# Linear attention and a mixture of experts on one core: the last batch's u projected behind o instead of behind v

## The chip, the cores and the metric

The kernel runs on one core of one Trainium2 chip. A core has five engines that run their own queues of instructions and wait for each other by semaphores: TensorE (matmuls and transposes, into PSUM), VectorE, ScalarE, GpSimd (POOL in the profile) and SyncE (SP, which here only starts DMA transfers). The metric is the device time of one execution in microseconds.

## What is computed

`x` is 4 batches of 512 tokens of 256 numbers, all float32. First comes a gated linear attention with 16 heads of 16, then a mixture of 8 experts of which each token uses 2. Cut to what matters:

```python
def attn(x):                      # x is the layernorm of the input
    q = elu(x @ Wqk + bqk)        # keys are the same: k = q
    v = silu(x @ Wv + bv)
    u = silu(x @ Wu + bu)
    kv = einsum('bhnd,bhne->bhde', k, v)
    out = einsum('bhnd,bhde->bhne', q, kv)
    out = layernorm(out, ln_g, ln_b)
    return (u * out) @ Wo + bo

def ffn(x):                       # x is a layernorm again
    top2 = top_k(x @ gate, 2)     # weights: softmax over the two
    inter = silu(x @ w0[e]) * (x @ w1[e])
    return sum of weight * (inter @ wo[e]) over the two experts e

x = x + attn(layernorm(x))
x = x + ffn(layernorm(x))
```

u is needed only in the product `u * out`, after the second layernorm of its batch.

## The kernel before

**Stages.** `attention(b)` (L255) is a generator that yields after each of its 15 stages, one generator a batch. The loop at L668 runs 28 steps. Batches begin at steps 0, 4, 8 and 12, so up to four batches are in work, each in another stage. The stages, with the names that the profile shows:

- 0: layernorm 1 of `x` (L239 to L246)
- 1: transposes `xTp`, copied by ScalarE to `xT` (L266)
- 2: `qp`, the q projection, Exp on ScalarE, elu on VectorE, giving `kT`
- 3: `vp` (L291), bias and Silu; then `up` (L305), the u projection: for each of two column halves, two matmuls with `xT` as moving operand into a PSUM tile of 128x512, and a Silu on ScalarE (L309) into `uT`
- 4: `knp` (L318), transposes of `kT` back, copied by VectorE (L321)
- 5: `kvp` (L329), times a mask of heads on VectorE (L333)
- 6: `op` (L343), copied by ScalarE to `o` (L347)
- 7: layernorm 2 of `o`
- 8: transposes `oTp`, evicted by ScalarE with gain and bias (L356), times `uT` on VectorE (L360), giving `yT`
- 9: `ap` (L368), the output projection, added to `x` by VectorE (L372); ScalarE's queue starts the store of `x` to `y` (L375)
- 10: layernorm 3, into `hn`; 11: transposes `hTp`, copied by ScalarE to `hT` (L398); 12: `lp` (L406), the gate logits
- 13: MAX8 and FIND_INDEX8 pick two experts a token (L416, L417); 14: `pos` (L430) counts rows by expert, and GpSimd scatters the rows of `hn` to DRAM, sorted by expert, `xg` (L453)

**Expert blocks.** Once batches 0 and 1 are sorted (step 19), `plan` computes on VectorE a table of 9 full blocks of 128 rows ("early"), with `tot` as its input (L462). From step 20 on each step also advances these blocks: SyncE fetches 128 rows from `xg` (L572, behind the loads of `w2` into the arena, L142, that wait for the arena's places), TensorE transposes them (`gp`, L583), ScalarE and VectorE copy the block's two weight matrices to a staging place (L594, ScalarE the first), TensorE runs `hp` (L602) and `eo` (L624), VectorE and GpSimd scale and add the result to `y` in DRAM. After the attention come 8 "last" blocks and 23 "full" ones, without attention beside them.

**Order.** The order of the text is only the start: when the program is built, a scheduler orders the instructions of each engine, so neighbouring stages of different batches are mixed. At run time each engine keeps its order. Silu and Exp stand in different function tables of ScalarE; a table load (`ACT_TABLE_LOAD`, `LoadActFuncSet` in the program) is put in wherever the needed table changes.

**Places.** Long-lived tiles lie in `arena`, 16 places of 128x1024 float32. `att(tag)` (L94) hands out places in turn; the tag "feat" has three, which `xT`, `yT` and `hT` of all batches share, in the order of their stages.

## Time and profile before

| | us |
|---|---|
| median of 3 runs (346.89 to 348.01) | 347.54 |
| the profiled execution | 338.75 |
| its span, first to last instruction | 337.0 |
| TensorE busy with matmuls in the span | 304.0 (90%) |
| VectorE, ScalarE, GpSimd busy | 155.5, 126.6, 114.3 |
| mean clock granted to TensorE | 0.969 of full |

The profile is of one execution, with times in microseconds from the first instruction. A line of the timeline gives start, length, engine, line of the kernel, operation, result and inputs, count, and in brackets the idle time before it with the instruction that ended it. A q behind an engine's name is its sequencer, which starts DMAs. The time of the profiled execution is not that of the unprofiled runs; only differences are carried from one to the other.

### The profile page before, as it was taken

Reading aid. Unit: us, or ns where it says so; the run is one execution under the profiler, and the core shown is the slowest. Engines: PE = TensorE matmul, PEld = TensorE weight load, DVE = VectorE, ACT = ScalarE, POOL = GpSimd, SP = SyncE. Lnnn points to the kernel's source line nnn. Section 1 sums busy time; section 2 is a strip of 40 time slices with the busy share of each in tenths; the row PEclk is TensorE's granted clock in tenths of the full one; section 3 lists DMA queues with packets and bytes.
Section 4 is the critical chain, followed back from the end, with each engine's and each line's share of the span. In section 5 each row is a group of like instructions: output and inputs, shape, how many; then the busy total and the mean of one; then the engine's idle time right before and its main releaser. Section 6 shows DMA issues by size and latency. Waiting matters only on the chain. (4 is left out here: it accounts for less than half of the span.)

```text
span 337.0 us, 5947 instructions
## 1 busy us (share of the span) xinstructions
PE 304.0 (90%) x2068; PEld 272.9 (81%) x2068; DVE 155.5 (46%) x525; ACT 126.6 (38%) x196; POOL 114.3 (34%) x146
## 2 busy tenths in 40 slices
PE   0999999899987879999999999999999999999930
PEld 0467687696777679999999999999999999999920
DVE  4855879779487665346212121323333232323110
ACT  1455828826613264543211121424243433334100
POOL 5410211307327267356333233232223223413230
PEclk9999999999996799999999999999999999999985
DMA  7999112035256642227434342323634434222220
GB/s 214 375 387 386 59 62 64 2 117 167 82 153 229 178 154 72 36 63 218 85 64 63 49 63 49 47 49 48 175 126 64 61 51 63 37 30 24 26 34 0
DMA packets 27871, 35.58 MB, mean 106 GB/s; under 512 B 2848, under 2 KB 22688, under 8 KB 27808
## 3 DMA queue, kind: packets, MB, share of 16 engines
q1 hardware_dynamic: 18960, 22.00, 21.1%
q0 software_dynamic: 6768, 11.08, 17.8%
q10 hardware_dynamic: 2112, 2.10, 1.9%
q8 instruction: 18, 0.29, 0.4%
q14 instruction: 13, 0.11, 0.1%
HBM read 22.89 MB, written 14.37 MB: 111 GB/s over the span
## 5 line engine op out<-in xcount | busy, mean ns | idle before, releaser
L602 PE MATMUL hp_full<-arena 128*128 128x128 f32 x608 | 73.9, 275 | 0.0
L602 PEld LDWEIGHTS hp_full<-arena 128*128 128x128 f32 x608 | 72.3, 192 | 1.0
L633 POOL DMA_INDIRECT out_dram<-ys_full,g_full x16 | 25.3, 1584 | 58.7 <-DVE ys_full L629 31.8
L453 POOL DMA_INDIRECT xg<-hn,idx_i x32 | 32.5, 1014 | 28.6 <-issue 11.1
L624 PE MATMUL eo_full<-arena,it_full 128*128 x152 | 36.1, 380 | 0.9 <-DVE it_full L612 0.9
L602 PE MATMUL hp_early<-arena 128*128 128x128 f32 x288 | 35.0, 275 | 1.7 <-ACT arena L594 1.7
L602 PEld LDWEIGHTS hp_early<-arena 128*128 128x128 f32 x288 | 34.1, 192 | 2.3 <-ACT arena L594 1.9
L602 PE MATMUL hp_last<-arena,w_sb 128*128 128x128 f32 x256 | 31.2, 275 | 0.0
L602 PEld LDWEIGHTS hp_last<-arena,w_sb 128*128 128x128 f32 x256 | 30.5, 192 | 0.4
L624 PEld LDWEIGHTS eo_full<-arena,it_full 128*128 128x128 f32 x152 | 27.4, 190 | 4.0 <-DVE it_full L612 1.0
L594 ACT COPY arena<-w_sb 128x1024 f32 x28 | 29.3, 1047 | 3.5 <-DVE idx_i L439 1.5
L629 DVE TENSOR_SCALAR ys_full<-eo_full,g_full 128x256 f32<-128x256 f32 x19 | 9.2, 484 | 45.2 <-PE eo_full L624 45.2
L586 ACT COPY arena<-gp_full 128x256 f32<-128x256 f32 x19 | 7.1, 372 | 59.6 <-PE gp_full L583 59.6
L261 POOL TENSOR_TENSOR x<-x,bo 128x256 f32<-128x256 f32 x16 | 12.1, 781 | 38.4 <-DVE arena L244 31.2
L612 DVE TENSOR_TENSOR it_full<-s_full,hp_full 128x512 f32<-128x512 f32 x19 | 13.1, 688 | 26.0 <-PE hp_full L602 26.0
L633 POOL DMA_INDIRECT y<-ys_early,g_early x9 | 14.4, 1597 | 22.7 <-issue 9.2
L633 POOL DMA_INDIRECT y<-ys_last,g_last x8 | 12.4, 1549 | 28.5 <-DVE ys_last L629 22.6
L368 PE MATMUL ap<-wo,arena 128*128 128x256 f32 x64 | 16.6, 414 | 3.9 <-DVE arena L360 2.4
L594 DVE COPY arena<-w_sb 128x1024 f32 x28 | 19.3, 690 | 1.3 <-issue 1.1
L368 PEld LDWEIGHTS ap<-wo,arena 128*128 128x128 f32 x64 | 12.9, 209 | 6.7 <-issue 3.1
L624 PE MATMUL eo_early<-arena,it_early 128*128 x72 | 17.1, 381 | 0.2 <-DVE it_early L612 0.2
L273 PE MATMUL qp<-arena,wqk 128*128 128x512 f32 x32 | 16.7, 668 | 0.2 <-ACT arena L266 0.2
(164 smaller groups left out, 456.7 us busy)
## 6 DMA issues: line engine op xcount, KB each, us to landing
w_sb<-in_w_dram SPq DMA_DIRECT2D x16, 512.0 KB, 10.8
arena<-in_w_dram SPq DMA_DIRECT2D x8, 512.0 KB, 4.6
g_full<-xg SPq DMA_DIRECT2D x19, 130.0 KB, 2.1
x<-in_x_dram SPq DMA_DIRECT2D x4, 512.0 KB, 5.5
y<-x ACTq DMA_DIRECT2D x4, 512.0 KB, 3.5
xg<-empty SPq DMA_DIRECT2D x9, 130.0 KB, 3.5
g_early<-xg SPq DMA_DIRECT2D x9, 130.0 KB, 2.4
g_last<-xg SPq DMA_DIRECT2D x8, 130.0 KB, 2.1
```

The costliest lines, as they stand in the source:

```text
L261: nc.gpsimd.tensor_tensor(xb[:, t, :], xb[:, t, :], bo_sb, ALU.add)
L273: nc.tensor.matmul(ps, lhsT=wqk_sb[:, k, bass.ts(c, P)], rhs=xT[:, k, :], start=(k == 0), stop=(k == EC - 1),)
L368: nc.tensor.matmul(ps[:, t - t0, :], lhsT=yT[:, c, bass.ts(t, P)], rhs=wo_sb[:, c, :], start=(c == 0), stop=(c == EC - 1),)
L453: apart(nc.gpsimd.indirect_dma_start(out=xg[:, :], out_offset=bass.IndirectOffsetOnAxis(ap=idx_i[:, t, k : k + 1], axis=0), in_=hn[:, t, k ...
L586: nc.scalar.copy(gT, ps)
L594: copy(w[i], hw_sb[i][:, bass.ds(at, OW)])
L602: nc.tensor.matmul(ps[:, m, :], lhsT=w[i][:, bass.ds(k * M + m * P, P)], rhs=gT[:, k, :], start=(k == 0), stop=(k == EC - 1),)
L612: nc.vector.tensor_tensor(it, s, ps, ALU.mult)
L624: nc.tensor.matmul(ps, lhsT=it[:, m, :], rhs=w2_sb[:, bass.ds(at + m * E, E)], start=(m == 0), stop=(m == MC - 1),)
L629: nc.vector.tensor_scalar(ys, ps, g[:, E : E + 1], None, ALU.mult)
L633: ins = nc.gpsimd.indirect_dma_start(out=whole[:, :] if full else y[:, :], out_offset=bass.IndirectOffsetOnAxis(ap=g[:, E + 1 : E + 2].bit ...
```

## The change

The body of the u projection becomes a local function `project`. Batches 0 to 2 call it where it stood, behind v (stage 3). Batch 3 (`LATE = 3`) calls it behind o (stage 6). So `xT` of batch 3 is read three stages longer, and its place must stay untouched: the places of the tag "feat" are now listed one by one in `FEAT`. In the order of the turns these are xT0, xT1, yT0, xT2, hT0, yT1, xT3, hT1, yT2, hT2, yT3, hT3.

```diff
+    LATE = 3
...
+    FEAT = [0, 1, 2, 0, 1, 2, 1, 0, 2, 0, 2, 1]
+
     def att(tag):

-        i = turns[tag] % COUNT[tag]
+        i = FEAT[turns[tag]] if tag == "feat" else turns[tag] % COUNT[tag]
         turns[tag] += 1
...
+        def project():
+
+            for c in range(EC):
+                ps = psum.tile([P, N], F32, tag="a", name=f"up_{b}_{c}")
+                for k in range(EC):
+                    nc.tensor.matmul(
+                        ps, lhsT=wu_sb[:, k, bass.ts(c, P)], rhs=xT[:, k, :],
+                        start=(k == 0), stop=(k == EC - 1),
+                    )
+                nc.scalar.activation(uT[:, c, :], ps, AF.Silu, bias=cols_sb[:, 1, c : c + 1])
...
-
         uT = att("uT").rearrange("p (c n) -> p c n", c=EC)
-        for c in range(EC):
-            ps = psum.tile([P, N], F32, tag="a", name=f"up_{b}_{c}")
-            for k in range(EC):
-                nc.tensor.matmul(
-                    ps, lhsT=wu_sb[:, k, bass.ts(c, P)], rhs=xT[:, k, :],
-                    start=(k == 0), stop=(k == EC - 1),
-                )
-            nc.scalar.activation(uT[:, c, :], ps, AF.Silu, bias=cols_sb[:, 1, c : c + 1])
+        if b < LATE:
+            project()
         yield
...
             nc.scalar.copy(o[:, t0 : t0 + 2, :], ps)
+        if b >= LATE:
+            project()
         yield
```

The number of matmuls and of VectorE, GpSimd and SyncE instructions that run stays the same; GpSimd and SyncE keep their order. In the built program the order of TensorE and ScalarE around the move changes so (batch numbers added; "table" is a table load):

```
TensorE before: vp3, up3, lp1, oTp2, knp3, ap2 and kvp3 mixed, pos1, op3, hTp2, tot, lp2, oTp3, ap3, gp, pos2, gp, hp, hp, hTp3, gp, hp
TensorE after:  vp3, lp1, oTp2, knp3, ap2, kvp3, pos1, op3, up3, hTp2, tot, lp2 and oTp3 mixed, ap3, gp, pos2, gp, hp, hp, hTp3 and gp mixed, hp

ScalarE before: table, v3, u3, oTp2, table, two1, store x2, op3, hn2, hTp2, o3, oTp3, two2, gp, store x3, weights, gp, hn3, weights, table, s, hTp3
ScalarE after:  table, v3, oTp2, table, two1, store x2, op3, hn2, table, u3, hTp2, o3, oTp3, table, two2, gp, weights, store x3, gp, table, s, hn3, weights, hTp3
```

ScalarE thus runs two table loads more. On VectorE both copies of knp3 now stand before the two products of batch 2 with u; of batch 3's statistics for layernorm 2, less stands before the end of batch 2's layernorm 3; and the first MAX8 of batch 2, which waits for lp2, stands in the middle of the plan of the early blocks, with the plan's rest and the products of batch 3 with u behind it.

## The prediction

> **What bounds the kernel now.** I read the page first: the 40 slices (8.4 us each), then the group of the work that moves.

> ```profile
> PE   0999999899987879999999999999999999999930
> ...
> PEclk9999999999996799999999999999999999999985
> ...
> L305 PE MATMUL up<-arena,wu 128*128 128x512 f32 x32 | 14.4, 592 | 0.0
> ```

> TensorE is the bound: nearly full from slice 1 to 37, except slices 11 to 14 (93 to 126 us), where its granted clock also falls to 6 and 7 tenths. The four u projections cost 14.4 us, 3.6 us a batch. The page's chain of waits names only the last scatter (0.4% of the span), so the reading must be by stage. I went to TensorE's timeline on both sides of the weak stretch (start, length, engine, line, operation, count, idle before and releaser).

> ```profile
> 83.73 3.60 PE L305 MATMUL up<-arena,wu 128*128 128x512 f32 x8
> 87.16 1.85 PE L406 MATMUL lp<-gate,arena 128*128 128x8 f32 x16
> 88.86 1.07 PE L252 MATMUL oTp<-ident,arena 128*128 128x128 f32 x8
> 89.77 1.04 PE L318 MATMUL knp<-ident,arena 128*128 128x128 f32 x8
> 91.19 1.10 PE L368 MATMUL ap<-wo,arena 128*128 128x256 f32 x4 [0.38 <-DVE arena L360]
> ...
> 97.53 2.03 PE L343 MATMUL op<-arena 128*128 128x128 f32 x16
> 102.60 1.07 PE L252 MATMUL hTp<-ident,hn 128*128 128x128 f32 x8 [3.04 <-DVE hn L244]
> 103.51 0.29 PE L462 MATMUL tot<-count,ones 128*128 128x8 f32 x2
> 104.23 3.64 PE L406 MATMUL lp<-gate,arena 128*128 128x8 f32 x16 [0.44 <-ACT arena L398]
> 107.73 1.95 PE L252 MATMUL oTp<-ident,arena 128*128 128x128 f32 x8
> 111.15 5.29 PE L368 MATMUL ap<-wo,arena 128*128 128x256 f32 x16 [1.47 <-DVE chosen L417]
> ...
> 119.64 3.84 PE L602 MATMUL hp_early<-arena 128*128 128x128 f32 x32 [1.70 <-ACT arena L594]
> ```

> To be seen: after batch 3's o (97.53), TensorE waits 3.04 us for batch 2's third layernorm. The same gate matmul then takes 3.64 us instead of 1.85, the transpose 1.95 instead of 1.07. From 119.64 on TensorE is full, so what counts is how much earlier the expert blocks start. Stretches of half a microsecond (length, busy time of each engine, clock, DMA share, GB/s) date the slow clock:

> ```profile
> 104.00:104.50 0.50, 0.27 (x2) 0.27 (x2) 0.50 (x4) 0.50 (x2) 0.50 (x1) 0.65 1.14 431
> 104.50:105.00 0.50, 0.50 (x4) 0.50 (x4) 0.50 (x5) 0.17 (x1) 0.40 (x1) 0.50 0.81 283
> ...
> 114.00:114.50 0.50, 0.50 (x3) 0.41 (x2) 0.00 (x0) 0.00 (x0) 0.00 (x0) 0.61 0.91 281
> ```

> Half clock from about 104.15 (0.65 = 0.3 at full, 0.7 at half) to 114.39: 10.24 us. Its price: gate 3.64-1.85 = 1.8, transposes 1.95-1.07 = 0.9, and 3.24 us of ap's 5.29 at half speed, 1.6. Together 4.3 us on the path into the blocks.

> [...] 10.24 us is 3.0 windows of 3.41. The window ending at 104.15 holds about 2.3 us of idleness (66%) and cost the clock. The one from 117.80, with 1.64 us idle (48%), did not. So the deciding idleness lies between 1.64 and 2.26 us; I take 1.95. [...] gate products and transposes from 62.3 to 66.87, with 1.07 us idle, did not lose it. [...] The trace shows only the load: below, 83.51 + 1.28 is followed by work at 84.80. I take 1.28 us[...].

> ```profile
> 83.51 1.28 ACT L299 ACT_TABLE_LOAD   x1
> 84.80 1.15 ACT L299 ACTIVATE arena<-vz 128x512 f32<-128x512 f32 x2
> 85.86 0.67 ACT L309 ACTIVATE arena<-up,cols 128x512 f32<-128x512 f32 x1
> ...
> 103.60 1.07 ACT L398 COPY arena<-hTp 128x512 f32<-128x512 f32 x2 [0.77 <-PE hTp L252]
> ```

> **The change, part by part.** Times are those of the profiled run (span 337.0, 338.75 us with what lies around it), up to 83.73 the same. The order on each engine is that of the built programs, and durations are those of the same rows now.

> *Taken out at 83.73:* 3.43 us of TensorE (87.16-83.73), and two Silus on ScalarE. Gate to 85.6, oTp to 86.5, knp to 87.4. Here not all is won. In the new VectorE order both knp copies (0.68 each, from 87.04) stand before the two products with u: products at 88.24 and 88.84. ap starts at 89.07, not 91.19: 2.1 us gained, 1.7 us now idle before ap. kvp ends near 94.5, pos starts 94.4 (was 96.50), op runs 95.4 to 97.4. Batch 2's index is ready 2.3 us earlier.

> *Layernorm 3 of batch 2.* It begins at 96.1 (var, was 98.59). Less of batch 3's statistics stand in between than before, so its nt ends at 98.85, not 101.65. The two ScalarE halves of hn end at 100.04.

> *Put in at 97.3:* u, 3.6 us, to 100.9, beside that layernorm. It fills the gap of 3.04 us; hn is ready 0.9 us before u ends, so hTp runs 100.8 to 101.8. On ScalarE, behind hn: one new table load 100.05 to 101.33, two Silus (0.68 each) to 102.65, and only then the copies of hT, to 103.24 and 103.72. This is the cost: the copies are 0.95 us earlier than at 103.60 instead of about 2. TensorE idles 1.25 us before the gate. The second new load (Exp, after the oTp evictions) lies beside VectorE's work; uncovered it would cost 1.28.

> *After that.* At full clock the gate ends 105.4, oTp 106.2, its eviction starts 106.15. VectorE's next wait matters:

> ```profile
> 107.92 0.17 DVE L416 MAX8 best<-lp 128x8 f32<-128x8 f32 x1 [1.24 <-PE lp L406]
> ...
> 110.31 0.69 DVE L360 TENSOR_TENSOR arena<-arena 128x512 f32<-128x512 f32 x1 [1.36 <-ACT arena L356]
> ```

> In the new order the first MAX8 stands in the middle of the plan, so some fourteen small operations behind it (about 2.0 us by their spacing now) wait for the gate: 105.45 to 107.43, then the product to 108.1. ap runs 108.25 to 111.95 (ended 116.44), after 2.05 us idle. SP's queue: the w2 load that waits for oTp goes at 106.3 (109.75), the first early fetch needs the plan's table (108.35) and a register load: 109.2 (110.94), landed at 112.2. The first block's transposes run at 112.25. Its ScalarE weight copy no longer stands behind the y store (issue 117.32, copy 118.54): 113.1 to 114.15. hp_early starts at 114.2, 5.4 us earlier. Then layernorm 3 of batch 3 (nt 117.6, hn on ScalarE to 118.8) stands before the second block's weight copy, 118.85 to 119.9: hp of block two at 119.95 instead of 124.41. That takes back 0.9; the small wait of 0.23 at 126.59 goes. From there TensorE is full, in the same order with the same instructions. Later fetches, scatters and stores keep their distances.

> *Feature places and uT.* Nothing. Each new predecessor was read long before: the last is hT3's, which is xT3, read by u until 100.9, written near 120. uT's place is overwritten by staging only after the product that reads it.

> Sum: 124.41-119.95 = 4.46, plus up to 0.2: 4.5 us, 334.3 by the profiled run. That run is 8.8 us under the median of the three shown (347.54); I carry the difference over: **343.0 us**. Two bounds: without the clock drop the old chain itself would reach block two near 124.41-4.3 = 120.1, so the gain is almost all clock. And a half-clock window in the new gaps costs 3.4/2 = 1.7.

> **The rivals.**
> 1. *The clock falls once all the same.* Of the new gaps, 2.05 us before batch 3's ap exceeds my threshold and 1.7 before batch 2's ap nears it. [...] 4.5-1.7 = 2.8 us: 344.7.
> 2. *Nothing measurable.* The timed runs before mostly kept the full clock: [...] shorter work in TensorE then only moves waits to VectorE and ScalarE. [...] Gain 0: 347.5. The same comes out if the idle stretch from 101.8 and thin work costs the clock up to ap (3.9 us back, 346.9).
> 3. *Slower: the drop moves into the new kernel.* The table load and Silus hold hT's copies, the plan waits behind the gate, and ap's gap grows to 2.05 us[...]. If most earlier runs had no drop and the new ones have one at that gap, 1.7 us is added: 349.2. It decides where fewer than half of the old runs lost the clock.

> **How the numbers follow.** Forecast 0.52 (range 341.8 to 344.2), rival 1 0.22, rival 2 0.14, rival 3 0.12. About 0.3% (1.0 us) can be told from no change. Faster: the first two, 0.74; same 0.14; slower 0.12. Range: a microsecond of my stage sums below the forecast, up to the edge of rival 2: 341.7 to 346.6.

> **What would show it.** Right: no wait above 1 us between op and up of batch 3, PEclk 9s in slices 13 and 14, batch 2's gate at 1.9 us, hp_early near 114 and equal gaps from there. Wrong: half clock from about 104 again, hp_early later than 117, or block two's weights much later than 120[...].

## The result

| | us |
|---|---|
| the kernel before, beside it | 347.88 (20 runs, 345.79 to 349.90) |
| the changed kernel | 351.38 (20 runs, 347.00 to 354.87) |
| ratio, without its 6 slowest runs | 1.0069 [1.0045, 1.0093] |
| forecast | 343.0 (341.7 to 346.6) |

Six of the 20 runs of the changed kernel are in a slower state, and without them it is slower by 0.7%, or 2.4 us (the medians of all runs differ by 3.5 us); the forecast had it 4.5 us faster. The profiled execution of the changed kernel took 353.07 us (span 351.3), one of its longer ones, so it serves only to show where to look; a shorter one, at 346.94 us, comes below. It looks unlike the profile of before in more than the place of u. The page, work in 40 slices (now of 8.8 us) and the granted clock:

```profile
PE   0999899899696988996999999999999999999930
...
PEclk9999999999896698999699999999999999999995
```

```profile
80.25 3.62 PE L305 MATMUL vp<-wv,arena 128*128 128x256 f32 x16
83.70 1.85 PE L415 MATMUL lp<-gate,arena 128*128 128x8 f32 x16
...
90.79 5.13 PE L377 MATMUL ap<-wo,arena 128*128 128x256 f32 x16 [3.27 <-DVE arena L369]
...
100.44 3.60 PE L293 MATMUL up<-arena,wu 128*128 128x512 f32 x8
103.88 1.04 PE L255 MATMUL hTp<-ident,hn 128*128 128x128 f32 x8
...
108.86 3.16 PE L415 MATMUL lp<-gate,arena 128*128 128x8 f32 x14 [1.74 <-issue]
111.87 1.52 PE L255 MATMUL oTp<-ident,arena 128*128 128x128 f32 x6
114.77 6.77 PE L377 MATMUL ap<-wo,arena 128*128 128x256 f32 x16 [1.38 <-DVE arena L369]
...
129.16 2.05 PE L611 MATMUL hp_early<-arena 128*128 128x128 f32 x16 [0.22 <-ACT arena L603]
```

To be seen: the move itself works. u stands at 100.44, hTp follows without a wait, and the wait of 3.04 us is gone. But batch 2's output projection waits 3.27 us and runs for the most part at half clock (5.13 instead of 3.7), the gate product is broken by 1.74 us, and batch 3's output projection takes 6.77. The second early block starts at 129.16, later than the 124.41 of the profile before. Why it waits is in the other engines' lines (DVE is VectorE, ACT is ScalarE), at 83 to 90 and at 167 us:

```profile
82.95 0.68 DVE L310 TENSOR_TENSOR vz<-vp,bv 128x512 f32<-128x512 f32 x1
87.21 0.69 DVE L310 TENSOR_TENSOR vz<-vp,bv 128x512 f32<-128x512 f32 x1 [3.58 <-PE knp L325]
87.82 0.16 DVE L425 MAX8 best<-lp 128x8 f32<-128x8 f32 x1
90.06 1.28 DVE L369 TENSOR_TENSOR arena<-arena 128x512 f32<-128x512 f32 x2
...
167.50 0.60 ACT L664 ACTIVATE s_early<-hp_early 128x512 f32<-128x512 f32 x1 [8.01 <-remote]
167.59 0.48 DVE L638 TENSOR_SCALAR ys_early<-eo_early,g_early 128x256 f32<-128x256 f32 x1 [5.64 <-remote]
```

The second vz needs only the v product, which ended at 83.87, and starts 3.3 us later. "remote" marks a wait that no instruction of the trace ended. The profile of before has no such wait. So there are two questions: does the change gain where these late starts are missing, and what do they cost each kernel?

### The profile page after: what moved, and what is told of

Same layout as the page of the kernel before. It is cut to its first block, busy times and chain, and to the rows that moved or that the text cites. A ratio compares the mean times of both kernels' runs of the same rounds, so it can differ in the third digit from the quotient of the medians.

```text
span 351.3 us, 5948 instructions
## 1 busy us (share of the span) xinstructions
PE 312.5 (89%) x2068; PEld 278.8 (79%) x2068; DVE 155.9 (44%) x525; ACT 129.0 (37%) x198; POOL 113.0 (32%) x146
## 5 line engine op out<-in xcount | busy, mean ns | idle before, releaser
L611 PE MATMUL hp_early<-arena 128*128 128x128 f32 x288 | 39.4, 292 | 3.7 <-issue 2.8
L462 POOL DMA_INDIRECT xg<-hn,idx_i x32 | 32.3, 1009 | 32.2 <-issue 11.1
L611 PEld LDWEIGHTS hp_early<-arena 128*128 128x128 f32 x288 | 37.6, 207 | 4.8 <-issue 3.1
L377 PE MATMUL ap<-wo,arena 128*128 128x256 f32 x64 | 19.3, 469 | 6.7 <-DVE arena L369 6.7
L377 PEld LDWEIGHTS ap<-wo,arena 128*128 128x128 f32 x64 | 15.0, 241 | 10.4 <-DVE arena L369 6.4
L638 DVE TENSOR_SCALAR ys_early<-eo_early,g_early 128x256 f32<-128x256 f32 x9 | 4.4, 484 | 29.3 <-PE eo_early L633 19.0
```

Of the source, the lines that this page charges most:

```text
L377: nc.tensor.matmul(ps[:, t - t0, :], lhsT=yT[:, c, bass.ts(t, P)], rhs=wo_sb[:, c, :], start=(c == 0), stop=(c == EC - 1),)
L462: apart(nc.gpsimd.indirect_dma_start(out=xg[:, :], out_offset=bass.IndirectOffsetOnAxis(ap=idx_i[:, t, k : k + 1], axis=0), in_=hn[:, t, k ...
L611: nc.tensor.matmul(ps[:, m, :], lhsT=w[i][:, bass.ds(k * M + m * P, P)], rhs=gT[:, k, :], start=(k == 0), stop=(k == EC - 1),)
L638: nc.vector.tensor_scalar(ys, ps, g[:, E : E + 1], None, ALU.mult)
```

## The experiments

Five groups of kernels ran, each group on one chip with the kernel before timed beside it. Ratios are to that kernel, with a 95% interval. The chips fall into two kinds. On three of them (groups 1, 3, 4) the kernel before takes 338.7 to 339.1 us, and no profile has a wait named remote: "prompt" below. On two (groups 2, 5) it takes 346.7 to 346.9, and every profile has them: "late". The profile that the forecast was read from is of the prompt kind. The profile of the changed kernel is of the late kind, and so are, by their times, the timed runs of both kernels in the result. Each chip appears in one group only, so whether the kind belongs to the chip or to the time of its group is not shown.

### Both kernels on both kinds of chip

No edit: the kernel before (first) and the changed kernel (the rest).

> The kernel before, once more, for a second trace of it. Clock theory (the old kernel's timed runs mostly keep the full clock where the first trace lost it): no half-clock stretch, or a short one, between 93 and 126 us, batch 2's gate at 1.9 us. Rival (the first trace is typical, the loss in the changed kernel lies elsewhere): again about 10 us at half clock from near 104. Either way some 9 us over the first trace's 337.0 us span have to show up as waits that the first trace lacks, since the timed runs stand at 347.9.

> The kernel before, for a profile beside the others of this group. Both theories: half clock of three or four windows between batch 3's o and batch 3's ap. If its time lies near 348 instead of 339, the theory that something outside the clock slows the timed runs (late completions on TensorE at the ends of GpSimd's groups of scatters) says that waits named remote or issue of several us appear here too, near 100 to 130 us; the theory of the clock alone says that only the granted clock is lower (under 0.95) and no such waits appear.

> The changed kernel, once more. Clock theory: half-clock stretches start in the waits ahead of batch 2's and batch 3's output projections (near 90 and near 108 us), 10 us or more in all. Table-load theory: full clock in this stretch, but hT's copies late behind the Silus and the product with u late behind the plan; blocks start at 119 or later even so. Stall theory: ScalarE and VectorE start several us after the TensorE result that they wait for, as in the first trace of the changed kernel (4.0 us before the plan's first operation).

> The changed kernel, timed. Clock theory: 0.985 to 0.993 of the kernel before wherever the profile shows no waits named remote; if such waits appear in the profile, 1.003 to 1.010 and a clock at least 0.01 below that of the kernel before.

> The changed kernel, for a profile beside the others of this group. Two kinds of profile have been seen. If waits named remote appear at the ends of GpSimd's groups of eight scatters (near 85, 105, 130 and 160 us), its span is near 345 to 351; if none appears, near 334.

> The changed kernel, for a profile beside the others of this group: span near 333 to 334 without waits named remote, 345 to 351 with them.

| | before | changed | |
|---|---|---|---|
| prompt, group 1 | 339.09 (27 runs) | 335.58 (1) | -3.5 |
| prompt, group 3 | 338.74 (43 runs) | 334.41 (1) | -4.3 |
| prompt, group 4 | 339.13 (19 runs) | 335.19 (1) | -3.9 |
| late, group 2 | 346.88 (57 runs) | 348.73 (20) | 1.005 [1.0028, 1.0073] |

On prompt chips the change gains about what was forecast. There are only single runs of it, but three, each below every run of the kernel before beside it (the lowest are 338.27, 338.25 and 338.56). On the late chip it loses, as before. A lower clock of the changed kernel was expected there, by 0.01 at least; that did not come: the median granted clock of both kernels' runs is 0.957. TensorE's timeline of the changed kernel on the first prompt chip:

```profile
79.50 3.62 PE L305 MATMUL vp<-wv,arena 128*128 128x256 f32 x16
...
88.15 3.72 PE L377 MATMUL ap<-wo,arena 128*128 128x256 f32 x16 [1.54 <-DVE arena L369]
...
99.83 1.04 PE L255 MATMUL hTp<-ident,hn 128*128 128x128 f32 x8
...
101.94 0.39 PE L415 MATMUL lp<-gate,arena 128*128 128x8 f32 x2 [0.95 <-ACT arena L407]
...
102.91 1.63 PE L415 MATMUL lp<-gate,arena 128*128 128x8 f32 x14
104.40 0.85 PE L255 MATMUL oTp<-ident,arena 128*128 128x128 f32 x6
107.95 6.05 PE L377 MATMUL ap<-wo,arena 128*128 128x256 f32 x16 [2.71 <-DVE arena L369]
...
121.65 2.05 PE L611 MATMUL hp_early<-arena 128*128 128x128 f32 x16 [0.26 <-ACT arena L603]
```

Here the waits come close to the forecast: before batch 2's ap 1.54 us (forecast 1.7), before and within the gate 0.95 and about 0.35 (1.25), before batch 3's ap 2.71 (2.05). Only that last ap shows half clock. Times from the start of batch 3's v product to later starts, from the same view of four profiles:

| us from v of batch 3 to | before, prompt | changed, prompt | before, late | changed, late |
|---|---|---|---|---|
| ap of batch 2 | 10.92 | 8.65 | 10.91 | 10.03 |
| gate of batch 2 | 24.49 | 22.44 | 23.95 | 23.80 |
| ap of batch 3 | 31.40 | 28.45 | 31.76 | 32.51 |
| second early block | 45.34 | 42.15 | 45.91 | 45.69 |
| fifth early eo | 72.82 | 69.10 | 74.47 | 74.51 |
| seventh early eo | 83.85 | 80.13 | 90.50 | 92.01 |

Prompt: 2.3 us gained at the first row, 3.2 at the second block, 3.7 from there on. Late: 0.9 at the first row, 0.2 at the second block and nothing at the fifth eo; then 1.5 is lost up to the seventh. The stretch from the fifth to the seventh eo takes 11.03 us in both prompt profiles, 16.03 in the late one of the kernel before (first fence) and 17.50 in that of the changed kernel (second). POOL is GpSimd, L453 or L462 its scatters:

```profile
154.29 1.89 PE L624 MATMUL eo_early<-arena,it_early 128*128 x8
...
158.30 0.98 POOL L453 DMA_INDIRECT xg<-hn,idx_i  x1 [0.30 <-issue]
...
160.53 0.38 PE L602 MATMUL hp_early<-arena 128*128 128x128 f32 x2 [1.09 <-issue]
161.96 3.00 PE L602 MATMUL hp_early<-arena 128*128 128x128 f32 x14 [1.04 <-issue]
162.01 0.60 ACT L655 ACTIVATE s_early<-hp_early 128x512 f32<-128x512 f32 x1 [7.82 <-remote]
162.10 0.48 DVE L629 TENSOR_SCALAR ys_early<-eo_early,g_early 128x256 f32<-128x256 f32 x1 [5.43 <-remote]
...
164.80 1.89 PE L624 MATMUL eo_early<-arena,it_early 128*128 x8
```

```profile
157.58 0.97 POOL L462 DMA_INDIRECT xg<-hn,idx_i  x1 [0.30 <-issue]
...
161.28 3.56 PE L611 MATMUL hp_early<-arena 128*128 128x128 f32 x15 [0.34 <-issue]
161.35 0.60 ACT L664 ACTIVATE s_early<-hp_early 128x512 f32<-128x512 f32 x1 [7.86 <-PE gp_early L592]
161.44 0.48 DVE L638 TENSOR_SCALAR ys_early<-eo_early,g_early 128x256 f32<-128x256 f32 x1 [5.47 <-PE gp_early L592]
...
164.64 2.83 PE L633 MATMUL eo_early<-arena,it_early 128*128 x8
```

VectorE's ys needs eo, which ended near 156.2 in the first fence, and starts at 162.10; TensorE runs single matmuls 0.7 to 1.4 us apart. In the second fence the profile names a transpose of TensorE (gp) as what ended the waits, but it had ended near 160.2, and the starts are the same late ones. The standstill costs both kernels alike: counted from batch 3's v, GpSimd's eight scatters begin after 69.3 and 69.4 us, and TensorE is through after 82.1 and 82.2. There is no head start left to lose at that point. What the changed kernel loses more is half clock: two windows instead of one (its eo takes 2.83 us instead of 1.89). This pair of profiles differs by 0.6 us in span, the medians of the runs on that chip by 1.9, so a part of the loss is in executions that no profile shows.

The first row of the table shows how the move uncovers a late start. On the late chip, the kernel before (two lines) and the changed kernel (two lines):

```profile
85.29 0.69 DVE L296 TENSOR_TENSOR vz<-vp,bv 128x512 f32<-128x512 f32 x1 [2.08 <-PE up L305]
90.73 1.10 PE L368 MATMUL ap<-wo,arena 128*128 128x256 f32 x4 [0.38 <-DVE arena L360]
...
84.59 0.69 DVE L310 TENSOR_TENSOR vz<-vp,bv 128x512 f32<-128x512 f32 x1 [2.11 <-PE oTp L255]
89.12 3.72 PE L377 MATMUL ap<-wo,arena 128*128 128x256 f32 x16 [2.92 <-DVE arena L369]
```

In both, VectorE's second vz starts 1.9 us after v's end (83.44 and 82.71). In the kernel before u keeps TensorE busy until 86.7, and batch 2's ap waits only 0.38 us. Without u there it waits 2.92 (1.54 on the prompt chip, 3.27 in the longer execution above). The rest of the gain goes at the gate: its second part waits 1.65 us for a late copy of hT, where the prompt profile has about 0.35.

### The table loads and Silus

The first kernel leaves out the Silu of batch 3's u and puts Identity in its place, so both new table loads fall away. The second holds the late Silus back behind hT's copies and the layernorm halves of batch 3. The edits are abridged:

```diff
-  nc.scalar.activation(uT[:, c, :], ps, AF.Silu, bias=...)
+  nc.scalar.activation(uT[:, c, :], ps, AF.Silu if b < LATE else AF.Identity, bias=...)
```

```diff
+  waiting.append((c, ps))
...
   layernorm(o, o, b, "2")
+  for c, ps in waiting:
+      tc.keep_in_program_order(nc.scalar.activation(uT[:, c, :], ps, AF.Silu, bias=...))
```

> The changed kernel with the late u left without its Silu (a plain bias instead), so that no function table is loaded for it: two table loads less on ScalarE. Table-load theory: 3 to 4 us faster than the changed kernel, at or below the kernel before (ratio to before 0.995 to 1.000). Clock theory: hT's copies come 1.3 us earlier and the waits in TensorE shrink by as much, 1 to 2 us faster than the changed kernel (ratio 1.002 to 1.006). If the loads cost nothing: ratio 1.007 as the changed kernel.

> The changed kernel with its two late Silus and their table load set behind the copies of batch 2's hT and behind batch 3's layernorm on ScalarE; the matmuls stay where they are. Table-load theory: the gate comes about 2 us earlier, 1.5 to 2.5 us faster than the changed kernel (ratio to before 1.000 to 1.003). Clock theory: the wait ahead of the gate goes, that ahead of batch 3's output projection stays; no more than 1 us faster (ratio 1.004 to 1.008).

On the first prompt chip: 336.39, 0.9908 [0.9880, 0.9935], and 338.16, 0.9967 [0.9951, 0.9984]; the changed kernel itself 335.58. Without the table loads hT's copies start 0.7 us sooner (100.89 in a profile in which v starts at 79.77, against 101.30 and 79.50), but TensorE then waits 1.05 us for batch 3's layernorm on VectorE, and batch 3's ap starts 28.57 us after v, against 28.45. So up to there the first new load costs nothing. The second stands in a wait as well: in the changed kernel it ends at 107.92, and ScalarE's next operation waits for VectorE until 109.38. The final times say less, since this version has a new wait further on (1.57 us instead of 0.64 before the first early block). Held back, the loads did not help, but for another reason: the eviction of oTp starts only 0.6 us later than in the changed kernel, counted from v, while the products of batch 3 with u start 1.8 us later, because the new order on VectorE puts batch 2's whole choice of experts ahead of them. The wait before batch 3's ap grows.

```profile
109.45 6.64 PE L390 MATMUL ap<-wo,arena 128*128 128x256 f32 x16 [4.55 <-DVE arena L382]
```

### Feature places alone, and half a move

`LATE = 4` leaves every u in its place and keeps the list of places. In the other kernel the first column half of batch 3's u goes back behind v:

```diff
-        if b < LATE:
-            project()
+        project(range(EC if b < LATE else 1))
...
-        if b >= LATE:
-            project()
+        if b >= LATE:
+            project(range(1, EC))
```

> The list of feature places alone: every u stays behind v. The forecast puts it at nothing: within 0.5 us of the kernel before, with the same half-clock windows. If a place that is reused too early held up the changed kernel: slower than the kernel before by more than 1 us, with a wait of ScalarE's copies or evictions on TensorE's reads.

> The changed kernel with the first half of batch 3's u (four matmuls, 1.8 us, and its Silu) back behind v and only the second half behind o. Theory: 1.8 us of work lie again ahead of batch 2's output projection, as cover for completions that come late in the first group of scatters (wait there under 0.8 us instead of 1.5 to 2.9), and 1.8 us still fill the wait of 3.04 us, leaving 1.2 us[...]. With late completions: 1 to 3 us less than the changed kernel, at or below the kernel before. Without them: within 1.5 us of the changed kernel. If the clock alone matters and the limit is lower than 1.2 us of idle: half clock from about 102 us as in the kernel before, and its time.

Places alone on a prompt chip: 338.71, 0.9998 [0.9985, 1.0011]: nothing, as forecast. Half a move: 339.78, 1.0026 [1.0010, 1.0042], a miss of what was expected without late completions (within 1.5 us of the changed kernel, 334.41), with four half-clock windows (102.06 to 115.71) like the kernel before. A new order brought a new wait: ScalarE does part of batch 3's layernorm ahead of hT's copies, and the gate product waits 2.98 us. It ran on a prompt chip only, so it says nothing of cover for late starts.

### A longer group of scatters

```diff
-        for t in range(NT):
+        for t in [0, 1, 2, 3] + ([0, 1] if b == B - 1 else []):
             for k in range(TOPK):
                 apart(nc.gpsimd.indirect_dma_start(
```

> The changed kernel in which GpSimd scatters the rows of two of batch 3's four token groups a second time, the same rows to the same places: 12 scatters in a row instead of 8, 1.3 us each, so 5.2 us more, right where the three other engines stood still (156 to 162 us). Nothing is left out. Theory of late completions during GpSimd's scatters: where the standstill is seen at all, it lasts 4 to 6 us longer and ends with the longer group, 2 us behind its end near 166 to 168; the kernel takes 4 to 6 us more than the changed one. Rival, that other traffic (the zero rows that SyncE stores from 154 us, or the instruction fetches) causes it: the standstill stays as long as it was, and what is lost is at most the wait for the rows of the first last block, under 3 us. Where no standstill is seen in the changed kernel, none here either.

> The changed kernel with 12 scatters of batch 3 in a row instead of 8 (5.2 us more, same rows to the same places). Where waits named remote appear in the changed kernel: the standstill of the three engines near 156 to 162 us lasts 4 to 6 us longer and ends about 2 us behind the longer group (late completions during scatters), or it stays as long as it was (other traffic). Where none appear: 0.5 to 1.5 us more than the changed kernel, from the wait for the first last block alone, as seen once.

335.94, 0.9926 [0.9902, 0.9951], and 335.43, 0.9885 [0.9861, 0.9909]: 1.5 and 0.2 us over the single runs of the changed kernel beside them, without any wait named remote. Both landed on prompt chips. Here four scatters more brought no late start; whether scatters cause it on late chips is not shown.

### Useless matmuls in the waits

`spin(ps, n)` puts n matmuls of 128x512 into a PSUM tile that is about to be overwritten, held behind what TensorE was given before. First version, three and five in the changed kernel (ahead of batch 2's and batch 3's ap), six in the kernel before (ahead of hTp):

```diff
+    def spin(ps, n):
+        for _ in range(n):
+            tc.keep_in_program_order(nc.tensor.matmul(
+                ps, lhsT=ident, rhs=wu_sb.rearrange("p c h -> p (c h)"), start=True, stop=True))
...
             ps = psum.tile([P, 2, E], F32, tag="a", name=f"ap_{b}_{t0}")
+            if t0 == 0:
+                spin(ps.rearrange("p t e -> p (t e)"), {2: 3, 3: 5}.get(b, 0))
```

> The changed kernel with useless matmuls of 128x512 (0.45 us each) in the two waits that the change opened: three ahead of batch 2's output projection, five ahead of batch 3's. Clock theory: no half-clock window between 85 and 120 us, batch 3's output projection 3.7 us instead of 6.05, and 1.5 to 2.5 us less than the changed kernel (332 to 334 where that takes 335.6; where that takes 351, 346 to 349). If the lost time is late completions rather than clock: the same as the changed kernel within 0.7 us, and the waits stay.

> The kernel before with six useless matmuls (2.7 us) in the 3.04 us wait between batch 3's o and batch 2's hT transposes; nothing else is added or left out. It prices the clock alone. The working of the forecast says that the whole old chain at full clock reaches the second early block near 120.1 instead of 124.41: 3.5 to 4.5 us less than the kernel before, as fast as the changed kernel or faster. If the waits and not the clock made up the gain: within 1 us of the kernel before.

> The changed kernel with three useless matmuls ahead of batch 2's output projection and five ahead of batch 3's (0.45 us each at full clock). Where no waits named remote appear: full clock from 85 to 120 us, batch 3's output projection 3.7 us instead of 5.7 to 6.05, and 1.5 to 2.5 us less than the changed kernel (332 to 333 where that takes 334.4). Where they appear: within 1 us of the changed kernel in the median, as seen once.

> The kernel before with six useless matmuls in its wait of 3.04 us. Clock theory, where no waits named remote appear: gate product of batch 2 1.85 us instead of 3.64, and 3.5 to 4.5 us less than the kernel before (334.2 to 335.2 where that takes 338.7), that is as fast as the changed kernel. If what the change gained came from work taken off TensorE's path and not from the clock: within 1 us of the kernel before.

| | late | prompt |
|---|---|---|
| changed, filled | 347.88, 0.9997 [0.9969, 1.0025] | 337.27, 0.9939 [0.9921, 0.9958] |
| before, filled | 347.38, 1.0026 [1.0005, 1.0046] | 338.88, 0.9992 [0.9973, 1.0012] |

They were mis-sized: one such float32 matmul is two records of 0.45 us, so 0.9 us; six of them held TensorE 5.3 us in a wait of 3. So none of the gains expected on prompt chips came, and the clock is not priced by them. On the late chip, though, the filled changed kernel is below the changed kernel as it is (0.9997 against 1.005, on the same chip, with intervals that do not meet), so filling its waits helps there; why is not shown. And one profile has a fall of the clock behind a window with little idle time. The changed kernel so filled, on the prompt chip, in stretches of half a microsecond:

```profile
101.50:102.00 0.50, 0.35 (x2) 0.30 (x2) 0.40 (x4) 0.50 (x2) 0.40 (x1) 1.00 0.20 58
102.00:102.50 0.50, 0.04 (x1) 0.03 (x1) 0.50 (x2) 0.50 (x2) 0.30 (x1) 1.00 0.23 83
102.50:103.00 0.50, 0.50 (x5) 0.50 (x6) 0.47 (x3) 0.50 (x2) 0.50 (x1) 1.00 0.62 216
...
105.00:105.50 0.50, 0.50 (x2) 0.15 (x2) 0.50 (x4) 0.49 (x1) 0.50 (x1) 0.54 0.76 266
```

Half clock from 105.04 for 3.41 us. In the window ahead of it, 101.63 to 105.04, TensorE was busy for all but some 0.5 us, with gate products of 8 columns (1.63+0.39) and transposes. That is far less idleness than the 1.95 us of the forecast.

Second version, sized to the waits, so that the order on all other engines stays: in the kernel before two ahead of hTp, one ahead of the gate, two ahead of batch 3's ap; in the changed kernel one ahead of each ap and one ahead of the gate.

> The kernel before with five useless matmuls of 0.9 us each, now of a size that fits the waits (the earlier version held TensorE 2 us too long): two in the wait of 3.04 us ahead of batch 2's hT transposes, one ahead of the gate product (wait 0.24 to 0.44, so up to 0.6 us of delay), two ahead of batch 3's output projection. The order on every other engine is that of the kernel before. Clock theory, where no waits named remote appear: no half clock between 100 and 115 us, gate product 1.85 us, output projection 3.7, and 3.0 to 4.3 us less than the kernel before, about the changed kernel's time. If the gain came from work taken off TensorE's path: within 1 us of the kernel before. Where waits named remote appear: a gain under 1.5 us.

> The changed kernel with three useless matmuls of 0.9 us, one in each of its waits ahead of batch 2's output projection, batch 2's gate product and batch 3's output projection; the order on every other engine is that of the changed kernel. Theory, revised by the last group: a window of 3.4 us without wide matmuls costs the clock, however little of it is idle; here no such window is left. Full clock from 85 to 115 us, batch 3's output projection 3.7 us instead of 5.7 to 6.05, and 1.0 to 2.3 us less than the changed kernel (333 to 334 where that takes 335.2). If the limit is idleness alone (1.95 us): the same, since the longest wait left is 1.8. If one wide matmul in a window is not enough: the half clock stays, within 0.5 us of the changed kernel.

On a late chip, against 346.67: before, filled, 344.86, 0.9961 [0.9943, 0.9979]; changed, filled, 345.40, 0.9973 [0.9947, 0.9999]. The filled kernel before:

```profile
102.50 1.09 PE L254 MATMUL hTp<-ident,hn 128*128 128x128 f32 x8 [1.22 <-DVE hn L244]
...
104.52 1.86 PE L419 MATMUL lp<-gate,arena 128*128 128x8 f32 x16
106.23 1.07 PE L254 MATMUL oTp<-ident,arena 128*128 128x128 f32 x8
107.14 1.88 PE L260 MATMUL ap<-wu,ident 128*128 128x512 f32 x4
111.96 3.72 PE L379 MATMUL ap<-wo,arena 128*128 128x256 f32 x16 [2.93 <-DVE arena L369]
...
123.61 1.95 PE L615 MATMUL hp_early<-arena 128*128 128x128 f32 x16
```

There is no half clock from 100 to 125 us: gate, transposes and ap take their full-clock times. It falls once afterwards, from 127.9 to 131.3, for one window. The second block comes 43.35 us after batch 3's v, against 45.91 on the other late chip. So there full clock alone, with u in its old place, is worth about 2.6 us at that point (two chips compared) and 1.8 in the end, a little more than the 1.5 that was expected at most with late starts.

The filled changed kernel did not reach the full clock that was expected of it:

```profile
106.21 3.15 PE L426 MATMUL lp<-gate,arena 128*128 128x8 f32 x14 [1.72 <-issue]
```

It runs at half clock from 106.06 to 112.88, two windows. The window before had about 0.8 us of the useless wide matmul in it, but 2.0 us of idleness, since the gate waited 1.72 us for a copy of hT that ScalarE started late (at 105.57). So the clock fell behind a window with one wide matmul in it, and the kernel's 345.40 is not its time at full clock. Both filled versions are below the kernel before on that chip, and so below the changed kernel as far as ratios from two chips can be compared (1.005). Neither sized version ran on a prompt chip: what full clock alone would bring there is still an argument, not a run. No version beat the changed kernel's 334.4 to 335.6 there.

## Why the prediction was wrong

- **The failed step: "That run is 8.8 us under the median of the three shown (347.54); I carry the difference over."** The 8.8 us were taken for an offset. They are mostly waits inside the program, in the stretch that the change touches and behind it. From the profile before on a prompt chip to that on a late one (spans 337.1 and 344.6), 0.7 us are lost ahead of batch 3's v, 0.6 from there to the second block, 1.1 to the fifth eo and 5.0 to the seventh. On prompt chips the kernel before takes 338.7 to 339.1 us, and the change gains 3.5 to 4.3; on the late chip it loses 0.5%, in the result 0.7%. So the rule that only differences are carried from the profiled execution to the others does not hold between the two kinds. Why some chips are late stays open.
- **u in front of oTp and knp, "2.1 us gained".** Right on prompt chips (2.3). On the late chip 0.9: u's 3.6 us had covered the late start of VectorE and ScalarE, which stands under the table above. The forecast put this at nothing, and the work that hid it was the work moved away.
- **The gap of 3.04 us, the table loads, the places.** The gap is gone in every profile. A table load took 1.28 us and, where nothing else held it up, the next operation stood 0.01 to 0.02 behind its end (84.80 behind 83.51 + 1.28). Neither load lengthened the way to batch 3's ap on the prompt chip (28.57 us after v without them, 28.45 with them). Places: 0.9998.
- **"So the deciding idleness lies between 1.64 and 2.26 us; I take 1.95."** Wrong. It was the author's estimate from two windows of one profile, and that idleness decides was not shown. In the first prompt profile of the changed kernel the clock falls at 105.87, behind a window with about 0.8 us of idleness. It falls for two windows (6.83 us) instead of none, and batch 3's ap takes 6.05. That is the forecast's first rival, one window longer than it was priced. The kernel before had four windows (13.65 us) in that chip's profile, not the three of the profile read, so the change saved two windows there instead of three. At the second block it gains 3.2 us and not 4.5, and it would be less if the kernel before had lost only what the profile read shows. That the sum came near the forecast on prompt chips is in part luck.
- **"hp_early starts at 114.2" and block two at 119.95.** With v 0.77 us earlier in the profile on the first prompt chip, that is 113.4 and 119.2; it measured 116.15 and 121.65, late by 2.7 and 2.5, mainly ap's 2.3 us of half clock and 0.7 us more of wait.
- **Slower.** The third rival said that the drop moves into the gaps of the new kernel. In the profile at 353.07 it does (5.13 and 6.77 us for the two ap), but the gaps are as long as they are because of late starts, which no rival had. In the execution at 346.94 the half clock around the move lasts three windows, against four in the kernel before on that chip, so in that execution the clock at the move is not what makes the changed kernel slower. Why its runs on late chips lose 0.5 to 0.7% at large stays open in part.

## What to carry to other kernels

Where the profiled execution and the timed runs differ by more than the expected gain, find the difference first: the profile may be of another kind of execution, and a stage read in it does not carry over by subtraction. Before work is moved out of a place, ask which waits of the other engines it covers there, also those that this profile doesn't show. And idle time alone did not tell here when TensorE's clock falls: it fell behind windows of 3.41 us with 0.45 and 0.8 us of idleness, and stayed full behind another with 0.8 us. Look at what runs in such a stretch, too.

## What was not expected of the hardware

- Two kinds of chip for one program, 338.7 to 339.1 us and 346.7 to 346.9. In all seven profiles of the slower kind the page gives no landing time for any transfer and some waits are named remote; in all thirteen of the other kind most landing times are there (2.0 to 2.1 us for the fetch of a full block, 130 KB) and no wait is named so. Whether the missing records and the late starts have one cause is open.
- On late chips ScalarE and VectorE start some 2 to 6 us after the end of the TensorE work that they need, near the ends of GpSimd's four groups of eight scatters: in the kernel before 85.29, 109.82, 132.42 and 162.10 us on VectorE; the groups end at 85.5, 108.4, 131.3 and 159.3. The first of them is the closest: in six of the seven late profiles the second vz of batch 3 starts 0.1 to 0.2 us before the end of the first group, in the seventh 1.3 us behind it. That is a coincidence in time, not a shown cause; the longer group of scatters did not meet such a chip. The last standstill has another candidate, since the issue of SyncE's eight stores of zero rows takes 8.2 us there, against 4.0 on the prompt chip; which is cause and which effect is open.
- Idle time does not sort the windows. The clock fell behind 101.11 to 104.52 on the second prompt chip, with 0.45 us idle, 1.1 us of transposes (32%) and the rest 8-column products. It stayed full behind 63.19 to 66.60 in the profile before (counted back from 104.15 in steps of 3.41), with 0.8 us idle, 2.0 us of transposes (58%) and the rest 8-column products, so not every window without wide matmuls lost the clock, against the theory of the last expectation. No run varied the share of transposes by itself; what lowers the clock is open.
